# Added rows kept in PSUM for the product with att, two shorter last batches, and one block as the last group of nodes

## The chip, the cores and the metric

The kernel runs on one core of a Trainium2 chip, in one launch. A core has TensorE (PE, with its weight loads shown apart as PEld), VectorE (DVE), ScalarE (ACT), GpSimd (POOL) and SyncE (SP), each with a queue of its own that it works through in order, and 16 DMA engines. The metric is the device time of an execution in microseconds; three runs are shown before, and one further execution was profiled.

## The reference

Two layers of message passing over a graph of 6250 nodes and 206250 edges sorted by destination (100000 edges, their reverses and a loop at each node), with a layer norm after each. The change lies in the first layer, GATv2 attention with 8 heads of 16 features:

```python
def gatv2(x, edge_index, edge_attr, W_l, b_l, W_r, b_r, W_e, att, b_att):
    src, dst = (edge_index[0], edge_index[1])
    xl = (x @ W_l + b_l).reshape(-1, H, O)
    xr = (x @ W_r + b_r).reshape(-1, H, O)
    ee = (edge_attr @ W_e).reshape(-1, H, O)
    m = jax.nn.leaky_relu(xl[src] + xr[dst] + ee, NEG_SLOPE)
    logits = jnp.einsum('eho,ho->eh', m, att)
    lmax = jax.ops.segment_max(logits, dst, num_segments=N)
    exl = jnp.exp(logits - lmax[dst])
    denom = jax.ops.segment_sum(exl, dst, num_segments=N)
    alpha = exl / (denom[dst] + 1e-16)
    msg = xl[src] * alpha[:, :, None]
    out = jax.ops.segment_sum(msg, dst, num_segments=N)
    return out.reshape(-1, H * O) + b_att
...
h = layer_norm(x + attn_out, g1, be1)
ffn = jax.nn.gelu(h @ W1 + b1, approximate=False) @ W2 + b2
return layer_norm(h + ffn, g2, be2)
```

The second layer gathers node features for each edge, multiplies them with filters made from edge attributes by a small network, and sums them by destination.

## The kernel before

**Tiling.** Edges are cut into 269 units of 768 (`TU` = 6 tiles of 128). For each unit, `load` (L394) has POOL gather six tiles of the source rows `xl` from the table `fXL` by indirect DMA (`gather`, L364), and SP load the edge attributes `ea`, the places `lb` and three rows `xr`. `xl` has 19 buffers. A head's 16 features stand beside a 17th column (`OW` = 17): the table's linear part, 0.2 of the sum over the features times att, so that leaky_relu's product with att is max(z, 0) times 0.8 att, summed over the features, plus that column.

**One unit's logits.** `terms(u, half)` (L413) lets PE add the edge term, the destination term and, for half 0 alone, the gathered rows (a product with the identity, L423) in a PSUM tile `z` of one half, three tiles. The pool `zp` has three such buffers (L387). Half 0 ends with an ACT copy of the linear column from `z` to `pr` (L426). `parts(u)` (L430) is DVE's: for half 0 the product max(z, 0) times `attb` from `z` to `pr` (L439); for half 1 first the sum of `z` and the gathered rows, written to `pr` (L436), then the product from `pr` to `pr` (L439). `logits` (L441) sums over the 17 columns.

**Batches.** Maxima by destination need scans along the edges, done for a batch of units at once with (unit, head) as partitions. Batches are of 3, 4 and 6 units and then of 8 (`HEAD`, `U`, `fast_plan` L57); each has an `end`, the step of its last unit's logits. `rows` transposes the logits (step end + 1), `peaks` scans (end + 2), `shifts` and `weights` make the exponentials (end + 3), and from step end + 4 on (end + 3 for the last batch) each of its units is given a step by the table `when` (L560): `messages` multiplies the rows by them on DVE, `sums` (one step later) sums them by destination on PE and has ACT copy the result to `sb` (L542, L543), `sum_up` and `collect` (two and three steps later) add it to `acc`. In the last 28 steps a step may take two units.

**Order.** The whole is under a manual schedule: each engine runs its instructions in the order in which the loop (L580 to L611) calls the functions. In step k that is: load(k + 2); terms(k + 1, 0); sum_up; terms(k + 1, 1); shifts and weights, or peaks, where due; sums; parts(k); places(k + 2), DVE's one-hot of the destinations; logits(k); collect; the one-hot and messages of the units of this step; rows where due; and a piece of the node work.

**Nodes.** When all edges into a group of node blocks (128 nodes each) are collected, `nodes` (L635) normalises them, runs the feed-forward network and three layer norms, and writes the second layer's table `fFEAT`. There are 25 groups for 49 blocks: one of one block, then 24 of two (`cuts`, L62). A group is a generator of 19 pieces; `Queue.step` (L93) advances the groups at work by one piece each, at most two groups (two lanes), the second counted from the first that hasn't ended. It is called once a step, twice from step 273 on; `rest` runs what is left after the last step. The second layer (`convolution`, L746) begins with a memset of its accumulator on POOL, in the place of `acc`, and with gathers from `fFEAT`.

Of the kernel before, what the change touches and what calls it, by code (L numbers as in the profile page):

```python
# [11 lines left out]
AF = mybir.ActivationFunctionType  # L12
OP = mybir.AluOpType
# [19 lines left out]
U = 8  # L33
# [4 lines left out]
H = 8  # L38
O = D // H
OW = O + 1  # L40
ZW = H * OW
G = 2
SPREAD = 6
HEAD = (3, 4)
RAW = 4
ENDING = 28
EB = 8
# [2 lines left out]
def fast_sizes(n_nodes, n_edges):  # L50
    nt = -(-n_edges // P)
    nu = -(-nt // TU)
    up = -(-nu // P) * P
    return nu, up, -(-(n_nodes + 1) // P) * P


def fast_plan(n, e):  # L57


    nu, _, np_ = fast_sizes(n, e)  # L60
    nb = np_ // P
    cuts = [0, *range(nb % G or G, nb + 1, G)]  # L62
    groups = [(b, c - b) for b, c in zip(cuts, cuts[1:])]
    done, need = [], [0] * nu
    for b, g in groups:
        q = min((b + g) * P / n, 1.0)
        u = min(nu - 1, int((q * e + SPREAD * math.sqrt(e * q * (1 - q))) / UE + 0.5))
        done.append(u)
        if u + 1 < nu:
            need[u + 1] = max(need[u + 1], (b + g) * P)  # L70
    head = HEAD if nu > sum(HEAD) else ()
    left = nu - sum(head)
    rest = (left % U,) if left % U else ()
    batches, u, end = [], 0, -2
    for m in head + rest + (U,) * (left // U):
        u += m
        end = max(u - 1, end + 2)
        batches.append((u - m, m, end))
    return groups, done, need, batches
# [28 lines left out]
class Fast:  # L108
# [88 lines left out]
    def tables(self, acc, xlp):  # L197
# [28 lines left out]
        with tc.tile_pool(name="tb1", bufs=1) as t1, tc.tile_pool(name="tb2", bufs=2) as t2, \  # L226
                tc.tile_pool(name="tbp", bufs=4, space=PSUM) as tp, \
                tc.tile_pool(name="trp", bufs=2, space=PSUM) as rp:
            xgs = []
            for u in range(min(RAW, NU)):  # L230
                xg = t1.tile([P, TU, D], F32, name="xg", bufs=RAW)
                for t in range(TU):
# [145 lines left out]
    def attention(self, acc, xlp, xls):  # L378
# [3 lines left out]
        tc, nc, a, NU = self.tc, self.nc, self.a, self.NU  # L382
        with ExitStack() as st:
# [7 lines left out]
            ohs, eas, zs, prs, lgs, ms, sbs, nds = {}, {}, {}, {}, {}, {}, {}, {}  # L391
            ws = {"last": (H, last)}

            def load(u):  # L394
                if u >= RAW:
                    xls[u] = xlp.tile([P, TU, ZW], F32, name="xl")
# [16 lines left out]
            def terms(u, half):  # L413
                ea, _, xr = eas[u]
                xl, oht = xls[u], ohs[u]
                z = zs[u, half] = zp.tile([P, 3 * ZW], F32, name="z")
                for lhs, rhs in ((ea, self.w3[:, 2]), (oht, xr)):
                    for t in range(3):
                        e = slice((3 * half + t) * P, (3 * half + t + 1) * P)
                        nc.tensor.matmul(z[:, t * ZW:(t + 1) * ZW], lhs[:, e], rhs,  # L420
                                         start=(t == 0 and lhs is ea), stop=(half == 1 and t == 2 and lhs is oht))
                if half == 0:
                    nc.tensor.matmul(z, self.ident, xl[:, :3, :].rearrange("p t f -> p (t f)"),  # L423
                                     start=False, stop=True)
                    prs[u] = wk.tile([P, TU * H, OW], F32, name="pr")
                    nc.scalar.activation(prs[u][:, :3 * H, O], z.rearrange("p (h o) -> p h o", o=OW)[:, :, O], AF.Copy)  # L426
                else:
                    del eas[u], ohs[u]

            def parts(u):  # L430

                for k in range(2):
                    z = zs.pop((u, k)).rearrange("p (h o) -> p h o", o=OW)
                    p = prs[u][:, 3 * H * k:3 * H * (k + 1)]
                    if k:
                        nc.vector.tensor_add(p.rearrange("p h o -> p (h o)"), z.rearrange("p h o -> p (h o)"),  # L436
                                             xls[u][:, 3:, :].rearrange("p t f -> p (t f)"))
                        z = p
                    nc.vector.scalar_tensor_tensor(p[:, :, :O], z[:, :, :O], 0.0, self.attb, op0=OP.max, op1=OP.mult)  # L439

            def logits(u):  # L441
                b, i = of[u]
# [46 lines left out]
            def shifts(b):  # L489

                R, hb, pk, cr = ws[b]
                gd = b1.tile([R8, UE], F32, name="gd")
                for s in (slice(0, UE // 2), slice(UE // 2, UE)):
                    nc.vector.scalar_tensor_tensor(gd[:R, s], hb[:R, s], cr[:R], pk[:R, s], op0=OP.add, op1=OP.max)
                sc = b2.tile([R8, 1], F32, name="sc")
                nc.vector.tensor_scalar(sc[:R], cr[:R], gd[:R, 0:1], 0.0, op0=OP.subtract, op1=OP.min)
                nc.scalar.activation(sc[:R], sc[:R], AF.Exp)
                sd = b2.tile([R8, U], F32, name="sd")
                nc.scalar.activation(sd[:R], self.bmask[:R], AF.Copy, scale=sc[:R])
                ws[b] = R, gd, sd  # L500

            def weights(b):
                R, gd, sd = ws[b]
                lg = lgs.pop(b)
                ex_ps = mp.tile([P, TU, R], F32, name="m")
                nc.tensor.matmul(ex_ps, self.ident, lg[:, :, :R], start=True, stop=False)
                for t in range(TU):
                    nc.tensor.matmul(ex_ps[:, t, :], gd[:R, t * P:(t + 1) * P], self.negi[:R, :R],
                                     start=False, stop=(t == TU - 1))
                ex = b2.tile([P, TU, R8], F32, name="ex")  # L510
                nc.scalar.activation(ex[:, :, :R], ex_ps, AF.Exp)  # L511
                for i in range(R // H):
                    xv = xls[self.batches[b][0] + i].rearrange("p t (h o) -> p t h o", o=OW)
                    nc.scalar.activation(xv[:, :, :, O], ex_ps[:, :, i * H:(i + 1) * H], AF.Exp)
                s_ps = mp.tile([P, U], F32, name="m")
                nc.tensor.matmul(s_ps, self.e128[:R], sd[:R], start=True, stop=True)
                s = b2.tile([P, U], F32, name="s", bufs=3)
                nc.scalar.activation(s, s_ps, AF.Copy)  # L518
                ws[b] = ex, s
# [37 lines left out]
                nc.vector.scalar_tensor_tensor(v, v, ws[b][1][:, i:i + 1], nds.pop(u), op0=OP.mult, op1=OP.add)  # L557


            when, ready, k = {}, 0, 0  # L560
            for u in range(NU):
                end = self.batches[of[u][0]][2]
                k = max(k, end + (4 if end < NU - 1 else 3))
                busy = {k - 2, k - 3} & {b[2] for b in self.batches}
                if len(when.get(k, ())) == (2 if k >= NU or k > NU - ENDING and not busy else 1):
                    k += 1
                when.setdefault(k, []).append(u)

            AHEAD = 2
            ends = {end: b for b, (_, _, end) in enumerate(self.batches)}  # L570
            for u in range(min(AHEAD, NU)):
                load(u)
                places(u)
            for half in range(2):
                terms(0, half)
            for k in range(max(when) + 4):
                now, sums_of, ups_of, got = (when.get(k - i, []) for i in range(4))
                if k + AHEAD < NU:
                    load(k + AHEAD)
                if k == 2:  # L580
                    nodes = Queue(self.nodes(st, acc), self.done, 2)
                if k + 1 < NU:
                    terms(k + 1, 0)
                if ups_of:
                    sum_up(ups_of)
                if k + 1 < NU:
                    terms(k + 1, 1)
                if k - 3 in ends:
                    shifts(ends[k - 3])
                    weights(ends[k - 3])  # L590
                if k - 2 in ends:
                    peaks(ends[k - 2])
                for u in sums_of:
                    sums(u)
                if k < NU:
                    parts(k)
                cs = [nc.vector.value_load(self.r0[0:1, u:u + 1], min_val=0, max_val=self.n) for u in got]
                if k + AHEAD < NU:
                    places(k + AHEAD)
                if k < NU:  # L600
                    logits(k)
                for u, c in zip(got, cs):
                    collect(u, c)
                for u in now:
                    ohs[u] = self.one_hot(wk, u)
                    messages(u)
                if k - 1 in ends:
                    rows(ends[k - 1])
                for _ in range(1 + (k > NU + 3) if k > 1 else 0):
                    nodes.step(max(got, default=-1))  # L610
            nodes.rest()  # L611
# [1024 lines left out]
```

## Time and profile before

| | us |
|---|---|
| runs | 4414.8, 4415.79, 4425.34 (median 4415.79) |
| the profiled execution | 4420.11, its span 4418.2 |
| first logits, last logits (L445) | 125.6, 2247.8 |
| gathers of the first layer | 45.3 to 2241.4 |
| first gather of the second layer | 2329.8 |

| engine | busy us over the span | share |
|---|---|---|
| PE | 3545.6 | 80% |
| DVE | 2581.9 | 58% |
| ACT | 963.3 | 22% |
| POOL | 3333.3 | 75% |

Times are counted from the start of the span. A row of the timeline has the start, the duration, engine, line, operation, what is written from what, a count, and in brackets the idle time of the engine before it with what ended it. A row of a group has the count, the busy time and the mean of one in ns, and the idle time before with its releasers. A row of waits has the total, the number and the longest. The chain of work that ended last is put down to POOL for 31%, to DMA and to PE for 20% each and to DVE for 11% of the span. Mean granted clock of TensorE: 0.829 of full speed.

### The profile page before, as it was taken

The page shows a single profiled execution, that of the slowest core. Times are in us where ns is not written, and L with a number is a line of the kernel's source. Part 1 is how long each engine was busy: PE and PEld are TensorE (multiplying, and loading weights), DVE is VectorE, ACT ScalarE, POOL GpSimd, SP SyncE. Part 2 cuts the span into 40 slices and gives each one's busy share as a digit, 9 for nine tenths or more (in the row PEclk, how much of TensorE's full clock was granted, in tenths as well). Part 3 has the DMA queues.
Part 4 walks back from the last instruction along what each step waited for, and adds up shares of the span by engine and source line. Part 5 has one row for each costly group of instructions (what it writes and reads, how often), then busy time and mean ns, then how long its engine had stood idle before and what let it go on. Part 6 is the DMA issues. An engine that isn't in the chain of part 4 may idle for free.

```text
span 4418.2 us, 67000 instructions
## 1 busy us (share of the span) xinstructions
PE 3545.6 (80%) x21381; PEld 2843.6 (64%) x21381; DVE 2581.9 (58%) x6023; ACT 963.3 (22%) x2528; POOL 3333.3 (75%) x3236
## 2 busy tenths in 40 slices
PE   7787777777677777777768888888888888888887
PEld 5665566566566656555646776677676767766776
DVE  5786676666676666666754444444444444444444
ACT  3122222222222222222242111111111211111111
POOL 6777777777777777777746777777777777777776
PEclk7787777888877787778778889888888888898987
DMA  7654444444444444444512222222222222222222
GB/s 206 176 153 120 130 129 124 128 131 127 127 128 126 129 130 127 126 123 132 134 42 64 60 60 57 60 61 59 61 59 61 61 59 57 59 61 61 60 60 49
DMA packets 290617, 428.21 MB, mean 97 GB/s; under 512 B 122701, under 2 KB 199455, under 8 KB 290255
## 3 DMA queue, kind: packets, MB, share of 16 engines
q0 software_dynamic: 103296, 218.27, 20.3%
q1 hardware_dynamic: 183258, 197.74, 14.9%
q10 hardware_dynamic: 3700, 7.82, 0.5%
q8 instruction: 173, 2.83, 0.3%
q14 instruction: 190, 1.55, 0.1%
HBM read 403.55 MB, written 19.96 MB: 96 GB/s over the span
## 4 chain that ended last, share of the span: by engine, by line
POOL 31%; DMA 20%; PE 20%; issue 15%; DVE 11%; ACT 1%; DVEq 1%; ACTq 0%; SPq 0%; POOLq 0%
POOL f L366 21%; DMA xl<-fXL,fsrc 10%; POOL xl L366 9%; DMA f<-fFEAT,fsrc 8%; PE z L420 6%; PE z L423 3%; DVE f L833 2%; PE m L538 2%; PE y L852 2%; PE m L551 1%; DVE f L829 1%; DVE pr L439 1%; DVE os L825 1%; PE y L850 1%; DVE xl L528 1%
## 5 line engine op out<-in xcount | busy, mean ns | idle before, releaser
L366 POOL DMA_INDIRECT xl<-fXL,fsrc x1590 | 1711.8, 1077 | 487.3 <-issue 401.9
L366 POOL DMA_INDIRECT f<-fFEAT,fsrc x1614 | 1577.2, 977 | 506.5 <-issue 443.7
L852 PE MATMUL y<-os,f 128*128 128x96 f32 x3228 | 774.8, 325 | 10.2
L850 PEld LDWEIGHTS y<-os,f 128*128 128x128 f32 x3228 | 551.3, 208 | 353.2 <-DVE f L833 301.5
L829 DVE TENSOR_TENSOR f<-w,f 128x256 f32<-128x256 f32 x405 | 171.6, 424 | 982.0 <-DMA f<-fFEAT,fsrc 973.2
L850 PE MATMUL y<-os,f 128*128 128x32 f32 x3228 | 583.5, 264 | 198.1 <-DVE f L833 197.7
L420 PE MATMUL z<-fw,ea 128*128 128x136 f32 x3228 | 622.6, 340 | 64.9 <-DVE pr L439 55.7
L803 ACT ACTIVATE h<-h_ps 128x384 f32<-128x384 f32 x540 | 265.2, 491 | 1647.1 <-PE h_ps L802 1647.0
L423 PE MATMUL z<-xl,fcst 128*128 128x408 f32 x538 | 317.0, 678 | 364.0 <-DMA xl<-fXL,fsrc 363.7
L420 PEld LDWEIGHTS z<-fw,ea 128*128 128x128 f32 x3228 | 535.1, 237 | 114.1 <-DVE pr L439 56.3
L852 PEld LDWEIGHTS y<-os,f 128*128 128x128 f32 x3228 | 538.5, 209 | 31.5 <-DVE f L833 30.6
L809 PE MATMUL w<-wq,h 128*128 128x256 f32 x1620 | 498.3, 437 | 0.0
L833 DVE TENSOR_TENSOR f<-w,f 128x384 f32<-128x384 f32 (+1 forms) x810 | 408.7, 546 | 0.0
L423 PEld LDWEIGHTS z<-xl,fcst 128*128 128x128 f32 x538 | 99.6, 231 | 390.2 <-issue 316.3
L809 PEld LDWEIGHTS w<-wq,h 128*128 128x128 f32 x1620 | 317.0, 217 | 30.8
L825 DVE TENSOR_TENSOR os<-oh,e 128x512 f32<-128x512 f32 x405 | 280.2, 692 | 64.6 <-PE y L852 26.7
L538 PE MATMUL m<-xl,oh 128*32 128x136 f32 x3228 | 226.9, 349 | 72.4 <-ACT s L518 55.3
L436 DVE TENSOR_TENSOR pr<-z,xl 128x408 f32<-128x408 f32 x269 | 154.7, 575 | 209.9 <-DMA xl<-fXL,fsrc 117.7
L528 DVE TENSOR_TENSOR xl<-xl,ex 128x384 f32<-128x384 f32 x538 | 273.6, 548 | 4.0 <-ACT ex L511 4.0
L551 PEld LDWEIGHTS m<-fcst,sb 128*128 128x128 f32 x1076 | 204.1, 240 | 109.5 <-issue 104.7
L445 DVE TENSOR_REDUCE lg<-pr 128x48 f32<-128x816 f32 x269 | 266.5, 991 | 1.8 <-DVE pr L439 1.8
L802 PE MATMUL h_ps<-h,m 128*128 128x384 f32 x540 | 263.0, 622 | 0.0
(145 smaller groups left out, 4152.8 us busy)
## 6 DMA issues: line engine op xcount, KB each, us to landing
ea<-fast_eat_dram SPq DMA_DIRECT2D x269, 384.0 KB
lb<-fLB SPq DMA_DIRECT2D x269, 144.0 KB
f<-fFEAT,fsrc POOLq DMA_INDIRECT x1614
xl<-fXL,fsrc POOLq DMA_INDIRECT x1590
xr<-fXR SPq DMA_DIRECT2D x807, 8.5 KB
e<-fast_e8t_dram SPq DMA_DIRECT2D x16, 384.0 KB
fXR<-pt SPq DMA_DIRECT2D x16, 306.0 KB
fXL<-tb SPq DMA_DIRECT2D x16, 204.0 KB
```

The source lines that it names most:

```text
L366: self.nc.gpsimd.indirect_dma_start(out=to, out_offset=None, in_=table, in_offset=bass.IndirectOffsetOnAxis(ap=self.src[:, g:g + 1], axis=0))
L420: nc.tensor.matmul(z[:, t * ZW:(t + 1) * ZW], lhs[:, e], rhs, start=(t == 0 and lhs is ea), stop=(half == 1 and t == 2 and lhs is oht))
L423: nc.tensor.matmul(z, self.ident, xl[:, :3, :].rearrange("p t f -> p (t f)"), start=False, stop=True)
L445: nc.vector.tensor_reduce(lgs[b][:, :, i * H:(i + 1) * H], prs.pop(u).rearrange("p (t h) o -> p t h o", h=H), axis=mybir.AxisListType.X, o ...
L528: nc.vector.tensor_mul(v, v, ws[b][0][:, t:t + 3, i * H:(i + 1) * H, None].to_broadcast([P, 3, H, O]))
L538: nc.tensor.matmul(ag[q * W:(q + 1) * W], oh[:, t, :], xl[:, t, :], start=(t < 4), stop=(t + 4 >= TU))
L803: nc.scalar.activation(h[:, s], ps, AF.Gelu_apprx_tanh, scale=sc)
L809: nc.tensor.matmul(w[:, 2 * t:2 * t + 2, :], hs[p][:, e:e + P], wq, start=True, stop=True)
L825: nc.vector.tensor_mul(os[:, own], oh.rearrange("p t u w -> p (t u) w")[:, own, None, :].to_broadcast([P, n, 4, W]), e4s[p][:, at, :, None ...
L833: nc.vector.tensor_mul(vy[:, :, j, 32:].rearrange("p t (c x) -> p t c x", c=3), w[:, :, None, 64 + j * 32:96 + j * 32].to_broadcast([P, n, ...
L850: nc.tensor.matmul(ys[p][:, i, 0], vy[:, e, 0], os[:, e, 3], start=(c == t == i == 0), stop=False)
L852: nc.tensor.matmul(ys[p][:, i, 1:], vy[:, e, 1], os[:, e, :3], start=False, stop=last)
```

## The change

In `parts`, DVE adds the gathered rows of half 1 to `z` in PSUM and writes the sum back there. The linear column of half 1 is then copied by ACT from `z`, as that of half 0 was (`linear`, now called for both halves), and both products read `z`. The last two batches are of 5 and 3 units (`TAIL`), so that 36 take the place of 35; the last one's `rows`, `peaks` and `weights` come a step earlier, counted from its end, than those of the others, and the table `when` is made accordingly. The last group of nodes has one block, the 24 before it two.

```diff
+TAIL = (5, 3)
...
-    cuts = [0, *range(nb % G or G, nb + 1, G)]
+    cuts = [0, *range((nb - 1) % G or G, nb, G), nb]
...
-    head = HEAD if nu > sum(HEAD) else ()
-    left = nu - sum(head)
+    head, tail = (HEAD, TAIL) if nu > sum(HEAD + TAIL) else ((), ())
+    left = nu - sum(head + tail)
     rest = (left % U,) if left % U else ()
     batches, u, end = [], 0, -2
-    for m in head + rest + (U,) * (left // U):
+    for m in head + rest + (U,) * (left // U) + tail:
...
-                    nc.scalar.activation(prs[u][:, :3 * H, O], z.rearrange("p (h o) -> p h o", o=OW)[:, :, O], AF.Copy)
+                    linear(u, 0)
...
+            def linear(u, k):
+
+                z = zs[u, k].rearrange("p (h o) -> p h o", o=OW)
+                nc.scalar.activation(prs[u][:, 3 * H * k:3 * H * (k + 1), O], z[:, :, O], AF.Copy)
+
             def parts(u):
 
+                z = zs[u, 1]
+                nc.vector.tensor_add(z, z, xls[u][:, 3:, :].rearrange("p t f -> p (t f)"))
+                linear(u, 1)
                 for k in range(2):
                     z = zs.pop((u, k)).rearrange("p (h o) -> p h o", o=OW)
-                    p = prs[u][:, 3 * H * k:3 * H * (k + 1)]
-                    if k:
-                        nc.vector.tensor_add(p.rearrange("p h o -> p (h o)"), z.rearrange("p h o -> p (h o)"),
-                                             xls[u][:, 3:, :].rearrange("p t f -> p (t f)"))
-                        z = p
-                    nc.vector.scalar_tensor_tensor(p[:, :, :O], z[:, :, :O], 0.0, self.attb, op0=OP.max, op1=OP.mult)
+                    nc.vector.scalar_tensor_tensor(prs[u][:, 3 * H * k:3 * H * (k + 1), :O], z[:, :, :O], 0.0,
+                                                   self.attb, op0=OP.max, op1=OP.mult)
...
-            when, ready, k = {}, 0, 0
+            when, k = {}, 0
+            due = {end + (end < NU - 1): b for b, (_, _, end) in enumerate(self.batches)}
             for u in range(NU):
                 end = self.batches[of[u][0]][2]
-                k = max(k, end + (4 if end < NU - 1 else 3))
-                busy = {k - 2, k - 3} & {b[2] for b in self.batches}
+                k = max(k, end + (4 if end < NU - 1 else 2))
+                busy = {k - 1, k - 2} & set(due)
...
-                if k - 3 in ends:
-                    shifts(ends[k - 3])
-                    weights(ends[k - 3])
-                if k - 2 in ends:
-                    peaks(ends[k - 2])
+                if k - 2 in due:
+                    shifts(due[k - 2])
+                    weights(due[k - 2])
+                if k - 1 in due:
+                    peaks(due[k - 1])
...
-                if k - 1 in ends:
-                    rows(ends[k - 1])
+                if k in due:
+                    rows(due[k])
```

More of the change, by code (lines that the diff above doesn't have):

```diff
@@ L569, in attention @@
             AHEAD = 2
-            ends = {end: b for b, (_, _, end) in enumerate(self.batches)}
             for u in range(min(AHEAD, NU)):
```

## The prediction

> **What bounds the kernel now.** I read the page's busy table first, then the groups of the first layer, then who waits for whom on DVE and PE between 300 and 2240 us, and last the order of time there and at the end of the layer. In the table by stretches the columns are the window, its length, then PE, PEld, DVE, ACT and POOL busy.
>
> ```profile
> 300.00:2240.00 1940.00, 1456.54 (x10074) 1157.57 (x10075) 1325.32 (x2990) 494.30 (x1577) 1510.24 (x1411) 0.80 0.47 127
> L366 POOL DMA_INDIRECT xl<-fXL,fsrc x1411 | 1511.6, 1071 | 430.1 <-issue 351.1 <-PE z L420 17.7 <-DMA xl<-fXL,fsrc 8.8
> PE z L423 <- DMA xl<-fXL,fsrc: 363.7, 154, 6.4
> PE z L420 <- DVE pr L439: 37.0, 25, 2.6
> DVE pr L439 <- ACT pr L426: 108.3, 82, 4.1
> ```
>
> POOL has 1411 gathers in 1940 us and never idles longer than its fixed 0.30 us between two: 1071 + 304 ns each, six to a unit, 8.25 us per unit. PE and DVE wait for what the gathers land (PE 363.7 us). So gathers set the pace, and the 235 steps (1411 / 6) cost DVE only 1325.32 / 235 = 5.64 us each. The fourth line says that the terms of unit k+1's second half wait for unit k's first product: `zp` has three buffers. The fifth says that a product of DVE waits for the ACT copy of the linear column of the same half, although the two write different columns; over the stage the shortest gap from the end of that copy to the product is 0.03 us.
>
> The order of one step, from the timeline:
>
> ```profile
> 1210.36 0.21 ACT L426 ACTIVATE pr<-z 128x24 f32<-128x24 f32 x1 [0.45 <-PE z L423]
> ...
> 1212.10 0.52 DVE L439 SCALAR_TENSOR_TENSOR pr<-z,fattb 128x384 f32<-128x384 f32 x1
> ...
> 1212.55 0.56 DVE L436 TENSOR_TENSOR pr<-z,xl 128x408 f32<-128x408 f32 x1
> ...
> 1212.68 1.20 PE L420 MATMUL z<-fw,ea 128*128 128x136 f32 x6 [2.05 <-DVE pr L439]
> 1213.15 0.56 DVE L439 SCALAR_TENSOR_TENSOR pr<-pr,fattb 128x384 f32<-128x384 f32 x1
> ...
> 1214.98 1.12 PE L538 MATMUL m<-xl,oh 128*32 128x136 f32 x12 [0.25 <-ACT cr L485]
> ...
> 1216.21 0.28 ACT L542 ACTIVATE sb<-m 128x128 f32<-128x128 f32 x1 [1.28 <-PE m L538]
> ```
>
> The second product (1213.15) follows the add at once, long before PE's sums of the step (1214.98) and ACT's `sb` copies (1216.21). Nothing on ACT holds DVE there.
>
> **The change, part by part.**
>
> *1. The add stays in PSUM.* Add, product, product replace product, add, product. The second product reads `z` instead of `pr`: by its sister's row 546 for 562 ns, -0.02 us. An add that writes PSUM is in no row. Its ends are the product from `z` over 384 columns (0.55) and the reduce over 816 (0.99); I take its own row with the other destination, 0.58, nearest in shape. The ends are worth -0.03 and +0.41 us a step.
>
> *2. A second copy of the linear column, on ACT: 0.21 us (row L426).* As busy time it is nothing, ACT being busy 494 of 1940 us. But its place decides. `linear(u, 1)` is called in `parts(k)`, after `sums` of the same step, and ACT runs in program order: it stands behind the two `sb` copies, these wait for PE's sums, these stand behind `terms(k+1, 1)`, and those wait for the first product of step k. The second product, behind the copy as L439 is behind L426 today, cannot start until all of it is through. On DVE everything else of the step is queued behind that product: the one-hot of unit k+2, logits, collect, one-hot, messages, the nodes' pieces, and the next add and first product, which release PE again. A ring closes in each step, and DVE idles in it between its two products for:
> - first product to PE 0.06 (1212.62 to 1212.68)
> - second half's terms 549.9 / 471 + 188.5 / 471 = 1.57 (groups L420 of 2826 and 1413, six and three a half)
> - sums 202.2 / 238 = 0.85 (group L538, 2856 = 238 x 12)
> - PE to ACT 0.11 (1216.10 to 1216.21), `sb` pair 0.44 (1216.21 to 1216.65; L543's row is 1216.38, 0.27), copy 0.21, ACT to DVE 0.03
>
> That is 3.27, less about 0.1 where PE's groups overlap: 3.2 us. A step with `weights` adds its PE and ACT work to the ring, from the groups of that window: 31.1 / 29 + 50.6 / 29 (L506, L508) + 0.48 + 1.70 + 0.17 (L511, eight of L514, L518) - 0.85 for the sums that run beside = 4.3 us, over 8 units 0.54. A step with `peaks` adds 0.84 (1214.14 to 1214.98), 0.10 a unit. One unit then takes 5.64 + 3.2 + 0.54 + 0.10 = **9.48 us, more than the gathers' 8.25**. The bound changes: POOL fills the four `xl` buffers that it has to spare (19 against 15 live) and then waits.
>
> The cover today is also worth something at the start: logits of unit 0 are at 125.6 us and those of unit 268 at 2247.8, 7.89 us a unit, because the first thirty steps run faster than the gathers on loads made ahead. That is lost too. New: 269 x 9.48 = 2550, less 22 for the seven steps among the first thirteen that have no sums (3.2 each) and 18 for 23 early steps without node work (206 us of DVE node groups / 269 = 0.77 each): 2510. Last logits at 2636 instead of 2248: **+388 us**.
>
> [...]
>
> *3. What POOL gains.* Counted over the timeline, 151 of the 1411 gathers begin while a second product runs, and together last 21.6 us more than at the median of 944 ns; beside the first product, which reads PSUM, the excess is nil. With POOL no longer the bound, this is worth nothing; if it stays the bound, -22 us. [...]
>
> *4. Batches of 5 and 3.* One batch more before the last logits: 4.0 of scans (L471 to L477), 1.2 of `shifts`, 4.3 + 0.8 in the ring, +10. After them, today:
>
> ```profile
> 2251.16 0.60 PE L462 MATMUL m<-fcst,lg 128*64 128x128 f32 x4
> ...
> 2263.65 1.03 DVE L528 TENSOR_TENSOR xl<-xl,ex 128x384 f32<-128x384 f32 x2 [4.05 <-ACT ex L511]
> ...
> 2293.68 21.23 POOL L761 MEMSET acc<- 128x6304 f32 x4 [52.26 <-PE n L676]
> 2329.81 0.95 POOL L366 DMA_INDIRECT f<-fFEAT,fsrc  x1 [14.90 <-DMA fBASE<-h]
> ```
>
> 12.5 us (2251.16 to 2263.65) pass with one batch alone; now messages of the five lie beside it, though its scans and weights still take about 9 in the same queues, and two steps fall away, one with work of its own: -5. From the last collect (ends 2292.1) to the second layer's first gather 37.7 us pass, through the last group's chain.
>
> *5. Last group one block.* The chain's PE, DVE and ACT pieces halve in width: two L702 of 2.08, L710 3.57, L733 2.07, three L632 of 0.88, statistics and adds: about -9.5. But the node queue has two lanes. By the new due units group 22 starts at step 267 and has 12 of its 19 pieces behind it when the steps end; group 24 may not start until it is through, seven rounds later. Sixteen rounds now take 31 us (2293.6 to 2324.6), so +13.6. Together +4. The memset (21.2 us) stays covered: it starts with the last group's first matmuls, and 22 us of chain and 5 of landing follow.
>
> **Sum:** 388 + 10 - 5 + 4 = +397 us; I take +390, since waits now in DVE's busy stretches may fall into the idle ones. The profiled execution has 4420.11 us (span 4418.2 and 1.9 around it), 4.3 above the median of the three runs, 4415.79: 4810 by the profile, **4805 by the median**.
>
> **Rivals.**
> *The ring stays open, or fits* (chance 0.12). If the product doesn't wait for the copy, or the ring is shorter than 8.25 us, gathers stay the bound: 4416 - 22 - 5 + 4 + 5 (the added batch, half hidden) = 4398, faster. It decides where a unit takes under 8.25, 1.2 less than my sum. For it: the idle time of DVE today, 2.6 us a step, is nearly the ring's 3.2. Against: the 108.3 us row, and in-order ACT.
> *A ring at full clock* (0.10). PE's granted clock is 0.80 in the stage. In the fast stretches the second half's terms take 1.12 (1230.51 to 1231.63) and sums 0.66: idle 2.5, weights 0.51, 8.73 a unit, 4620. For it: PE will be less busy. Against: stretches with less PE work had no higher clock (0.66 from 2240 to 2330).
> *Only the tail counts* (0.03): the two layers as before, tail -1 to +8: 4416 to 4424.
> *A dear PSUM add* (0.05): +0.41 a step, 4915. Half clock throughout would be 10.4 a unit and 5050.
>
> **How the numbers follow.** My forecast has 0.70, 4660 to 4910. The range takes in the full-clock rival and the dear add: 4600 to 4930, about 0.83. This kernel can be told from no change at some 0.3%, 13 us. Faster 0.10, same 0.04 (the last two near-unchanged cases and the unlucky edge of the first), slower 0.86.
>
> **What would show it.** Right: the copy twice as often (538); the second product waiting for ACT some 3 us per step; PE's 363.7 us of waits for gathers nearly gone; POOL idle beyond 0.30 us, released by PE's sums; POOL's share in the first layer down from 78% to about 68%; last group's first matmuls some rounds after the last collect. Wrong: POOL still without a wait, a unit in 8.25 us or less, or a second product that starts right behind the first.

## The result, and the profile after

| | before | after |
|---|---|---|
| median of four runs, us | 4417.93 (4414.80 to 4425.34) | 4888.34 (4874.83 to 4906.12) |
| ratio | 1 | 1.1064 (95%: 1.1021 to 1.1108) |
| span of the profiled execution, us | 4418.2 | 4895.2 |
| first logits, last logits, us | 125.6, 2247.8 | 116.2, 2723.8 |
| one unit, from the logits of unit 60 to those of unit 240, us | 8.28 | 9.98 |
| last logits to the second layer's first gather, us | 82.0 | 91.7 |
| from there to the end, us | 2088.4 | 2079.7 |

The change costs 470 us. Between the two profiles the span grows by 477.0: the stretch from the first to the last logits by 2607.6 - 2122.2 = 485.4, the piece after it by 9.7, while the time before the first logits and the second layer take 9.5 and 8.7 less. The last two are not the change's: a second pair of executions on another chip (the last experiment) has 115.0 before and 117.2 after for the first, 2082.1 and 2080.5 for the second. So the loss lies in the first layer's steps.

The table by stretches of the kernel after, with the columns as in the prediction:

```profile
300.00:2600.00 2300.00, 1618.43 (x9926) 1252.87 (x9924) 1303.47 (x2950) 521.41 (x1780) 1496.74 (x1392) 0.71 0.39 107
```

At 9.98 us a unit, 2300 us are 230.4 steps. POOL is busy 65% of them (78% before), DVE 1303.47 / 230.4 = 5.66 us a step, as before (5.64). PE's granted clock is 0.71, where it was 0.80. The groups of the same stretch, kernel after:

```profile
L367 POOL DMA_INDIRECT xl<-fXL,fsrc x1392 | 1496.7, 1075 | 806.0 <-ACT pr L434 399.4 <-issue 329.6 <-ACT sb L548 12.4
L421 PE MATMUL z<-fw,ea 128*128 128x136 f32 x2796 | 609.3, 371 | 509.9 <-DVE pr L443 500.2 <-issue 9.4
L443 DVE SCALAR_TENSOR_TENSOR pr<-z,fattb 128x384 f32<-128x384 f32 x466 | 256.3, 551 | 945.1 <-ACT pr L434 942.7 <-issue 2.4
L543 PE MATMUL m<-xl,oh 128*32 128x136 f32 x2784 | 210.6, 366 | 16.9 <-ACT s L523 7.2 <-ACT cr L490 6.9 <-ACT sb L548 2.9
L421 PE MATMUL z<-xr,oht 96*128 96x136 bf16 x1398 | 205.5, 269 | 0.0
L439 DVE TENSOR_TENSOR z<-z,xl 128x408 f32<-128x408 f32 x232 | 134.3, 579 | 0.8 <-PE z L424 0.4
L434 ACT ACTIVATE pr<-z 128x24 f32<-128x24 f32 x466 | 98.8, 212 | 418.1 <-PE z L424 345.7 <-DVE h L719 21.3 <-DVE xl L533 12.6
```

The gathers last as long as before (1075 ns for 1071), but POOL now idles 806 us beside them. The add that writes PSUM takes 579 ns; the one that wrote SBUF took 576. Waits of the same stretch, kernel after (total, number, longest):

```profile
DVE pr L443 <- ACT pr L434: 942.7, 229, 11.4
ACT sb L547 <- PE m L543: 668.1, 229, 8.0
PE z L421 <- DVE pr L443: 500.2, 330, 7.8
POOL xl L367 <- ACT pr L434: 399.4, 115, 16.3
```

Read from the top: once a step (229 of 230) DVE waits with a product for ACT's copy of the linear column; ACT waits with its `sb` copies for PE's sums; PE waits with the terms for a product of DVE. That is a closed ring. PE's wait for gathered rows, 363.7 us before, no longer appears. POOL waits for the ring; by the profile its long waits end with ACT's column copy. One turn of it in the timeline of the kernel after:

```profile
1224.86 0.54 DVE L443 SCALAR_TENSOR_TENSOR pr<-z,fattb 128x384 f32<-128x384 f32 x1
1225.45 1.73 PE L421 MATMUL z<-fw,ea 128*128 128x136 f32 x6 [3.67 <-DVE pr L443]
1226.97 0.55 PE L421 MATMUL z<-xr,oht 96*128 96x136 bf16 x3
...
1228.29 1.12 PE L543 MATMUL m<-xl,oh 128*32 128x136 f32 x12 [0.25 <-ACT cr L490]
...
1229.46 0.28 ACT L547 ACTIVATE sb<-m 128x128 f32<-128x128 f32 x1 [1.22 <-PE m L543]
1229.63 0.27 ACT L548 ACTIVATE sb<-m 128x128 f32<-128x128 f32 x1
1229.79 0.22 ACT L434 ACTIVATE pr<-z 128x24 f32<-128x24 f32 x1
1230.04 0.56 DVE L443 SCALAR_TENSOR_TENSOR pr<-z,fattb 128x384 f32<-128x384 f32 x1 [4.64 <-ACT pr L434]
```

The first product ends at 1225.40, PE starts the next unit's second half 0.05 us later, then come two small products of a step with `peaks`, the sums, the two `sb` copies, the column copy, and 0.03 us after it the second product. Three engines take turns, and DVE stands still for 4.64 us.

The end of the layer, kernel after:

```profile
2768.10 0.60 DVE L562 SCALAR_TENSOR_TENSOR acc<-acc,s,m 128x64 f32 x2 [1.31 <-issue]
...
2785.09 0.39 PE L680 MATMUL n<-fcst,acc 128*128 128x8 f32 x2 [0.93 <-DVE h L742]
2785.75 21.23 POOL L766 MEMSET acc<- 128x6304 f32 x4 [137.89 <-PE n L681]
2815.50 0.95 POOL L367 DMA_INDIRECT f<-fFEAT,fsrc  x1 [8.52 <-issue]
```

Everything is collected at 2768.70; the last group's first products start only 16.4 us later, released by a node instruction of another group (L742). Before, the memset that follows these products started 1.6 us after the last collect (2292.1 to 2293.7).

### The profile page after: what moved, and what is told of

Its sections match the earlier page's. It is cut to its first block, busy times and chain, and to the rows that moved or that the text cites. A ratio compares the mean times of both kernels' runs of the same rounds, so it can differ in the third digit from the quotient of the medians.

```text
span 4895.2 us, 67029 instructions
## 1 busy us (share of the span) xinstructions
PE 3763.0 (77%) x21407; PEld 2978.3 (61%) x21407; DVE 2578.7 (53%) x6030; ACT 1004.2 (21%) x2805; POOL 3323.3 (68%) x3236
## 4 chain that ended last, share of the span: by engine, by line
POOL 19%; issue 8%; DVE 8%; DMA 8%; PE 7%; ACT 1%; DVEq 1%; POOLq 0%; ACTq 0%
POOL f L367 19%; DMA f<-fFEAT,fsrc 8%; DVE f L838 2%; PE y L857 1%; PE z L421 1%; DVE f L834 1%; DVE os L830 1%; PE m L543 1%; PE y L855 1%; DVE xl L533 1%; PE ps L916 1%; DVE pr L443 1%; DVE lg L450 1%; PE w L814 1%; PE h_ps L807 0%
## 5 line engine op out<-in xcount | busy, mean ns | idle before, releaser
L367 POOL DMA_INDIRECT xl<-fXL,fsrc x1590 | 1705.6, 1073 | 899.2 <-ACT pr L434 421.8
L421 PE MATMUL z<-fw,ea 128*128 128x136 f32 x3228 | 700.7, 370 | 602.6 <-DVE pr L443 567.5
L421 PEld LDWEIGHTS z<-fw,ea 128*128 128x128 f32 x3228 | 587.4, 258 | 711.0 <-DVE pr L443 611.4
L443 DVE SCALAR_TENSOR_TENSOR pr<-z,fattb 128x384 f32<-128x384 f32 x538 | 295.8, 550 | 1072.0 <-ACT pr L434 1069.5
L424 PE MATMUL z<-xl,fcst 128*128 128x408 f32 x538 | 340.9, 726 | 0.0
L807 PE MATMUL h_ps<-h,m 128*128 128x384 f32 x540 | 280.4, 658 | 0.0
L533 DVE TENSOR_TENSOR xl<-xl,ex 128x384 f32<-128x384 f32 x538 | 273.0, 546 | 0.0
L543 PE MATMUL m<-xl,oh 128*32 128x136 f32 x3228 | 245.3, 369 | 22.9 <-ACT s L523 8.4
L421 PE MATMUL z<-xr,oht 96*128 96x136 bf16 x1614 | 236.6, 268 | 1.5 <-DVE pr L443 1.2
```

The source lines that it names most:

```text
L367: self.nc.gpsimd.indirect_dma_start(out=to, out_offset=None, in_=table, in_offset=bass.IndirectOffsetOnAxis(ap=self.src[:, g:g + 1], axis=0))
L443: nc.vector.scalar_tensor_tensor(prs[u][:, 3 * H * k:3 * H * (k + 1), :O], z[:, :, :O], 0.0, self.attb, op0=OP.max, op1=OP.mult)
L533: nc.vector.tensor_mul(v, v, ws[b][0][:, t:t + 3, i * H:(i + 1) * H, None].to_broadcast([P, 3, H, O]))
L543: nc.tensor.matmul(ag[q * W:(q + 1) * W], oh[:, t, :], xl[:, t, :], start=(t < 4), stop=(t + 4 >= TU))
```

## The experiments

One caution first. The first four runs, the next four and the two after them were made on three other chips, on which the kernel before itself took 5399, 5352 and 5404 us (19, 35 and 17 runs). There a unit takes 9.4 to 9.7 us even where no ring closes (9.66 with `copy_first`). Ratios below are always to the kernel before on the same chip, and are the estimates on record with their 95% intervals, which are not exactly the quotients of the two medians (5699.24 / 5398.93 is 1.056, the estimate 1.0597). The times in us that the first expectations name were meant for a kernel before of 4418 us; on these chips only ratios and waits can be set against them. What is different on these chips is taken up at `loose_ring`.

**The products alone (psum_alone) and the plan alone (plan_alone).** The first is the change's hunks in `terms` and `parts`, the second all the others.

```diff
+                z = zs[u, 1]
+                nc.vector.tensor_add(z, z, xls[u][:, 3:, :].rearrange("p t f -> p (t f)"))
+                linear(u, 1)
```

```diff
+TAIL = (5, 3)
...
+    cuts = [0, *range((nb - 1) % G or G, nb, G), nb]
...
+            due = {end + (end < NU - 1): b for b, (_, _, end) in enumerate(self.batches)}
```

> The kernel before with the edit of parts alone: add into PSUM, ACT copy of half 1's column, both products from z; batches and groups as before. Ring theory (the second product waits for a copy that stands on ACT behind the sb copies of the step): nearly the whole loss stays, 4860 to 4890 us, DVE idle before the product from z by some 4 us per step, released by ACT. Plan theory (the batches of 5 and 3 and the last group cost the time): 4410 to 4425.

> The kernel before with the batches of 5 and 3, the earlier last batch and the last group of one block, and parts as before. Ring theory: the first layer keeps the pace of the gathers (8.25 us a unit) and only the end changes, -5 to +15 us, 4413 to 4433. Plan theory: 4850 to 4890.

The products alone: 5699.24 us for 5398.93, ratio 1.0597 (1.0548 to 1.0647), 10.78 us a unit. The plan alone: 5406.46, ratio 1.0032 (1.0004 to 1.0061). The loss is the products'. It is smaller than expected: 300 us here, where nearly all of 470 had been expected, since a unit takes longer here without the ring, too. Groups and waits between 600 and 2600 us, products alone:

```profile
L438 DVE TENSOR_TENSOR z<-z,xl 128x408 f32<-128x408 f32 x185 | 107.1, 579 | 0.7 <-PE z L423 0.3
```

```profile
DVE pr L442 <- ACT pr L433: 811.8, 154, 11.4
```

2000 us are 185.5 steps: 811.8 / 185.5 = 4.4 us a step of DVE waiting for ACT, in the same place, and again a PSUM add of 579 ns.

**The same with the copy at another place in ACT's queue (copy_first).** The add and the copy are called at the head of the step, so that the copy stands on ACT ahead of the `sb` copies.

```diff
-            def parts(u):
+            def added(u):
                 z = zs[u, 1]
                 nc.vector.tensor_add(z, z, xls[u][:, 3:, :].rearrange("p t f -> p (t f)"))
                 linear(u, 1)
+
+            def parts(u):
...
+                if k < NU:
+                    added(k)
```

> As psum_alone, but the add and the copy of half 1's column are called first in the step, ahead of the next unit's terms, so that on ACT the copy stands ahead of everything of its step; the operations and their number are the same. Ring theory: the ring is open, gathers set the pace again, less what POOL gains where the second product no longer reads two operands from SBUF (21.6 us by my count): 4385 to 4420. PSUM theory (an add that writes PSUM, or two products that read it beside PE, are themselves dear): stays at 4800 or more.

5384.10 us, ratio 0.9972 (0.9939 to 1.0005), 9.66 us a unit: the loss is gone on this chip, with the same instructions and the same PSUM add. The add has moved to the head of the step together with the copy; in `column_by_dve`, below, it stays where it was. Waits between 600 and 2600 us:

```profile
DVE pr L445 <- ACT pr L433: 316.6, 85, 13.0
```

DVE's wait for ACT falls from 4.4 to 316.6 / 207 = 1.5 us a step. A repetition on a third chip gave 0.9981 (0.9956 to 1.0005), 5392.60 for 5404.35:

> The earlier run of this kernel (the added rows stay in PSUM, and the column copy goes to ACT ahead of its copies of the sums; old plan of batches and groups) was on a chip where the kernel before took 5399 us, and its ratio was 0.9972. This run asks whether that holds where the gathers bound the first layer, as in the profile of before (8.28 us a unit, POOL 76%). Ring theory (the copy's place in ACT's queue closes the ring, nothing else in the product edit costs): the loss of 390 us is gone; at a kernel before of 4418 us this one takes 4390 to 4425 (ratio 0.994 to 1.002), a gain at most the 22 us that the gathers lose beside the old second product. PSUM theory (a slower add or product in PSUM): DVE's step stays longer by 0.1 to 0.3 us, the ratio is 1.00 to 1.02 with DVE's wait for ACT gone. Capacity theory (the copy on ACT is late whatever its place): ratio above 1.05.

It was meant to show whether the 22 us that gathers lose beside the old second product come back. It cannot: this chip, too, was one where the gathers don't bound the layer. Both intervals hold 1, so no version measured here is faster than the kernel before, and what `copy_first` does at 4418 us, whether it gains or even gets back all of the 470 us, was not measured.

**The ring without PSUM (ring_in_sbuf).** The add goes to `pr` in SBUF, as before, but ACT copies two columns of it onto themselves (258 ns for the 212 of the one column) ahead of the second product, at the place where the change has its copy; the product must wait for ACT with no write to PSUM by DVE.

```diff
+                p = prs[u][:, 3 * H:]
+                z = zs[u, 1].rearrange("p (h o) -> p h o", o=OW)
+                nc.vector.tensor_add(p.rearrange("p h o -> p (h o)"), z.rearrange("p h o -> p (h o)"),
+                                     xls[u][:, 3:, :].rearrange("p t f -> p (t f)"))
+                nc.scalar.activation(p[:, :, O - 1:], p[:, :, O - 1:], AF.Copy)
```

> The add goes to pr in SBUF as before and the second product reads pr as before, but the add stands ahead of both products and ACT copies two columns of pr in place (features 15 and the linear one) between add and second product, at the place that the new column copy has. Nothing writes PSUM but PE. Ring theory: the ring closes the same, 4830 to 4910, pace 9.6 to 10 us a unit. PSUM theory: as before, 4410 to 4430.

5678.95 us, ratio 1.0542 (1.0481 to 1.0602), 10.72 us a unit, on the same chip as the products alone (10.78). Waits between 600 and 2600 us:

```profile
DVE pr L440 <- ACT pr L436: 822.4, 155, 11.0
POOL xl L366 <- ACT pr L436: 468.4, 144, 11.1
```

Nearly all of the loss is there without the PSUM add. The theory that PSUM accesses are dear falls; a wait at this place is enough.

**The whole change with the copy first (change_copy_first), and the column copied by DVE (column_by_dve).** The first adds the diff of `copy_first` to the change. The second has the products of the change with DVE in ACT's place, so that no copy of the second half crosses engines:

```diff
-                linear(u, 1)
+                zv = z.rearrange("p (h o) -> p h o", o=OW)
+                nc.vector.tensor_copy(prs[u][:, 3 * H:, O], zv[:, :, O])
```

> The changed kernel whole, but with the add and the copy of half 1's column called first in the step, as in copy_first. Ring theory: the loss is gone; what is left is the plan's part (0 to +0.4%, the last group waits for a lane) less POOL's gain (0 to -0.5%): ratio 0.995 to 1.004. If the plan and the PSUM edit only cost together: 1.05 or more.

> As psum_alone (batches and groups as before), but DVE itself copies half 1's linear column from z, between add and products, some 0.1 to 0.3 us a unit; ACT has no second copy. Ring theory: no engine but DVE stands between add and second product, the ring is open, ratio 0.993 to 1.003. PSUM theory: as psum_alone, 1.05 or more.

5355.64 for 5351.61, ratio 1.0009 (0.9984 to 1.0034), and 5358.08, ratio 1.0012 (0.9976 to 1.0048). On this chip, either way of taking the copy out from behind the sums removes the whole loss. One more DVE instruction a step (199 ns in its group) costs nothing that can be told here.

**The two halves of the plan (groups_alone, batches_alone).** First the one block as the last group, with the old batches; then the batches of 5 and 3 with their due steps, with the old groups.

```diff
+    cuts = [0, *range((nb - 1) % G or G, nb, G), nb]
```

```diff
+TAIL = (5, 3)
...
+            due = {end + (end < NU - 1): b for b, (_, _, end) in enumerate(self.batches)}
```

> The kernel before with only the cuts changed (last group of nodes one block). Lane theory (a group may start only when the group before the last has ended): the last group starts 3 rounds of the rest after the last collect, some 6 us late, and is some 9 us shorter: -6 to +3 us at the end, ratio 0.998 to 1.001; its first matmuls (L676) come 4 to 8 us after the last collect. Without a lane effect they come at once, as in the kernel before, and the end is 9 us shorter.

> The kernel before with only the batches of 5 and 3 and the earlier last batch; cuts as before. From last logits to last collect 4 to 10 us less than before (44.2 us), last group's first matmuls at most 3 us after the last collect; against it one more batch before the last logits (0 to +10). Ratio 0.998 to 1.002.

Groups: 5357.18, ratio 1.0018 (0.9996 to 1.0041); batches: 5368.20, ratio 1.0027 (1.0006 to 1.0048). The end of the layer with the groups alone:

```profile
2774.36 0.60 DVE L557 SCALAR_TENSOR_TENSOR acc<-acc,s,m 128x64 f32 x2 [1.30 <-issue]
...
2785.79 0.29 PE L675 MATMUL n<-fcst,acc 128*128 128x8 f32 x2
2785.94 0.31 PE L676 MATMUL n<-fcst,acc 128*128 128x128 f32 x1
2786.36 21.23 POOL L761 MEMSET acc<- 128x6304 f32 x4 [111.05 <-PE n L676]
```

From the end of the last collect to the memset pass 11.4 us with the groups alone, 8.5 with the batches alone, 17.0 with both (the plan alone), and 1.0 with neither (`copy_first`). I had expected the last group's first products 4 to 8 us after the collect with the groups alone (2785.79 - 2774.96 = 10.8) and the start within 3 us with the batches alone. The batches alone were also expected to bring the last collect 4 to 10 us nearer to the last logits than the 44.2 us of the kernel before; it is 45.5. Each half of the plan alone delays the last group; neither gains anything.

**The copy where only the reduce waits for it (loose_ring).** The kernel before, with a copy of the same column after the second half's add, in place. Both products go ahead; the sum over the columns has to wait for ACT.

```diff
                         z = p
+                        nc.scalar.activation(p[:, :, O], p[:, :, O], AF.Copy)
                     nc.vector.scalar_tensor_tensor(p[:, :, :O], z[:, :, :O], 0.0, self.attb, op0=OP.max, op1=OP.mult)
```

> The kernel before, with one more ACT copy of the second half's column (in place, after the second product, of what the sum over the columns reads): only the reduce at the end of the products waits for it, not the second product. Ring theory: a copy of the same size, late in the same queue of ACT, costs little where the second product doesn't wait for it, since the ring then spans the reduce and its followers alone: 8.3 to 8.9 us a unit where the kernel before has 8.28, ratio 1.00 to 1.03. Rival (any more work of ACT between the two products costs the same, as ACT's queue itself is the bound): ratio 1.05 to 1.10, as with the product edit alone (1.06).

5592.31 for 5404.35, ratio 1.0371 (1.0319 to 1.0423), 10.39 us a unit: between the two bands, so both expectations miss. The timeline:

```profile
1239.71 0.57 DVE L436 TENSOR_TENSOR pr<-z,xl 128x408 f32<-128x408 f32 x1
...
1240.31 0.56 DVE L440 SCALAR_TENSOR_TENSOR pr<-pr,fattb 128x384 f32<-128x384 f32 x1
...
1242.59 0.66 PE L539 MATMUL m<-xl,oh 128*32 128x136 f32 x12
...
1245.89 0.28 ACT L543 ACTIVATE sb<-m 128x128 f32<-128x128 f32 x1 [4.30 <-PE z L420]
1246.07 0.27 ACT L544 ACTIVATE sb<-m 128x128 f32<-128x128 f32 x1
1246.22 0.24 ACT L439 ACTIVATE pr<-pr 128x24 f32<-128x24 f32 x1
...
1246.50 1.00 DVE L446 TENSOR_REDUCE lg<-pr 128x48 f32<-128x816 f32 x1 [5.07 <-ACT pr L439]
```

The second product follows the add at once (1240.28 to 1240.31), though ACT's copy into another column of the same `pr` is still to come: writing `pr` together makes no wait. In the change, the product and the copy also share `z`, and there the product waits (942.7 us in 229 waits). By elimination, that leaves the shared PSUM tile as the reason; why sharing it puts the two in order was not shown.

The ring is not open, though. The reduce waits, and with it all that stands behind it in DVE's queue, the next first product among it, which releases PE:

```profile
DVE lg L446 <- ACT pr L439: 858.3, 190, 9.8
```

Between 600 and 2600 us these are 192.5 steps, so DVE waits 858.3 / 192.5 = 4.5 us a step, as long as with the products alone. What is gained is the second product, which now goes ahead of the wait. A unit takes 10.39 us where it takes 9.68 with the copy first on the same chip (`copy_first_again`), 0.71 more; the products alone cost 10.78 - 9.66 = 1.12.

The rest of the turn shows what is different on these chips. PE's last recorded matmul of the sums ends at 1243.25, and ACT starts the `sb` copy only at 1245.89, 2.64 us later. Counted between 300 and 2200 us, the pair starts more than 1 us after both the sums and ACT's previous instruction in 116 of 182 steps of this run, 316.8 us in all or 1.74 a step. The seven other runs on these chips, in which no ring closes, have it as well: 50 to 59% of the steps and 2.2 to 2.7 us a step (493.4 us over 196 steps in `copy_first`). With the second product in the ring it is less, 62.5 us over 175 steps with the products alone and 98.5 over 176 with the ring in SBUF. In the kernel before and the kernel after, on the chips where the former takes 4418 or 4409 us, it never happens. In the waits of `copy_first` between 600 and 2600 us it stands as one that the profile can put down to nothing ("remote"):

```profile
ACT sb L549 <- remote: 392.3, 48, 20.0
```

In one such stretch PE has no record from 748.3 to 761.8 us, while POOL's gathers go on, most of them 1.25 us apart. These late starts can't be subtracted from a unit: `copy_first` would be left with 9.66 - 2.52 = 7.1 us, less than its six gathers take, 6 x (1.07 + 0.30) = 8.2. So these chips tell which place of the copy closes a ring, but not what a ring costs where the gathers are the bound. Whether the sums end later there than the records say, or their signal arrives later, isn't settled.

**Both kernels once more (change_again, before_again).**

> The whole change, unaltered, on a chip where the kernel before takes about 5400 us, beside which the parts were run. If the parts add (product edit alone 1.0597, plan alone 1.0032): ratio 1.063 (1.055 to 1.071), and 10.7 to 10.9 us a unit in the first layer, since the ring is the same and only the floor under it is higher here. Rival: the parts strengthen one another (the ring met by last batches of other sizes), as the first measurement's 1.106 would have it if it held on every chip: ratio 1.09 to 1.11.

> The kernel before, unaltered, for its trace on such a chip. If the floor is higher here because every step of the first layer loses time to waits that the ring does not cause, the unit is 9.5 to 9.8 us (as with the copy placed first, 9.66) instead of 8.28, the gathers' mean stays at 1.06 to 1.09 us, POOL is idle between gathers for over 900 us instead of 484, and second-layer time is 2500 us instead of 2088. Rival: the gathers themselves are slower here: their mean is 1.25 us or more and POOL is as full as before (over 75%).

Neither expectation could be tested, since this chip ran the kernel before in 4408.98 us (7 runs). It gave a second measurement of the result instead: 4881.41 us (4 runs), ratio 1.1054 (1.1014 to 1.1094); a unit 9.93 for 8.25. Waits between 600 and 2600 us, kernel after on this chip:

```profile
DVE pr L443 <- ACT pr L434: 812.2, 199, 11.1
PE z L421 <- DVE pr L443: 439.0, 285, 7.8
```

The first execution has 821.4 and 437.8 us there. Whether the parts add up to the whole cannot be checked on one chip from these runs: the parts were measured where a unit costs 9.66 us without the ring, the whole where it costs 8.28.

## Why the prediction was right, and where its sizes were off

**What bounds the kernel, and the ring.** Right. The forecast was that the column copy, in order behind the sums, closes a ring through DVE, PE and ACT and takes the bound from the gathers. The profile has its waits, and the copy's place in ACT's queue decides: 1.0597 behind the sums, 0.9972 ahead of them, the same instructions on the same chip. One sign came otherwise: POOL's waits were to be ended by PE's sums, and the profile puts them down to ACT's column copy (399.4 us).

**The length of a unit** is the term that was mis-sized: 9.48 us forecast, 9.98 measured. The parts, with the 230.4 steps of the stretch:

| us a step | forecast | measured |
|---|---|---|
| DVE's own work | 5.64 | 1303.47 / 230.4 = 5.66 |
| DVE's wait for ACT at the second product | 3.2 + 0.54 + 0.10 = 3.84 | 942.7 / 230.4 = 4.09 |
| DVE's other idle time | 0 | (2300 - 1303.47 - 942.7) / 230.4 = 0.23 |

Of the 0.25 us in the wait, PE explains most: by the groups above the terms of one half now take (609.3 + 205.5) / 466 = 1.75 us instead of 1.57, and the sums of a unit 210.6 / 232 = 0.91 instead of 0.85. I had priced PE's part at the clock of before (0.80), and the new schedule was granted 0.71. The 0.23 us, 54 in the stretch, are for the most part (43 us) gaps of under 0.15 us between DVE's instructions, which a sum of busy times leaves out.

**The early steps.** 40 us were taken off for steps without sums or node work; 268 x 9.98 - 2607.6 = 67 us is what the unit's steady pace overstates. So the last logits come 476 us later than before, not 388.

**The PSUM add** was put at the duration of the SBUF add, 0.58 us a step, between -0.03 and +0.41 of cost. It takes 0.579, and the ring without it costs nearly the same (1.0542 for 1.0597, with overlapping intervals): the value taken was right and the rival of a dear add falls.

**Full clock** was given a tenth, because PE would be less busy. The opposite came: 0.71. The reason given against it, that less PE work had not meant a higher clock before (0.66 from 2240 to 2330 us), was the right one to weigh more.

**An open ring** falls with the same lines. **Only the tail counts** falls with the 470 us.

**POOL's gain** of 21.6 us, called worth nothing if POOL is no longer the bound, went to nothing in another way, too: the gathers' mean is 1073 ns over the layer for 1077 before. Beside the products, which now read PSUM, the 264 gathers that begin there last 946 ns, but 212 begin beside the messages (L533, two inputs from SBUF) and last 1571 ns.

**The plan** was put at +10 - 5 + 4 = +9 us. The added batch (+10) ahead of the last logits can't be told from the ring. The piece behind them is 9.7 us longer (9.2 in the second pair of profiles), where -1 had been forecast:

| us | before | after | change, forecast | change, measured |
|---|---|---|---|---|
| last logits to last collect | 44.2 | 44.9 | -5 | +0.7 |
| last collect to memset (wait for a lane) | 1.6 | 17.0 | +13.6 | +15.4 |
| memset to first gather (the last group's chain) | 36.1 | 29.8 | -9.5 | -6.4 |

That the last group would wait for a lane was right, and nearly its size. The 5 us that the shorter last batches were to save never came, and the narrower chain saved two thirds of what was forecast. The plan alone costs 0.32% (0.04 to 0.61%) on its chip. What was not seen is that the batches alone make the last group wait as well.

**The sum.** Between the profiles it is 477 us for 397 forecast. The stretch of the logits is 97 us longer than forecast and the end 11; the added batch's 10 don't show, and the start and the second layer took 18 us less, which is luck, since it isn't the change's.

## What to carry to other kernels

A small instruction is not priced by its duration but by what stands ahead of it in its engine's queue: a 0.21 us copy behind two copies that wait for PE cost 9.98 - 8.28 = 1.7 us a step. Issued ahead of them it cost nothing that could be measured, on chips where a step takes 9.66 us anyway. Where an engine is 25% busy and "free", ask what the last instruction ahead of the new one waits for, and whether that comes back to the consumer of the new one; if it does, add up the whole turn and compare it with the pace of today's bound. A plan that gives the last stage less work gains only if the stage can also start: look for the lane, not only for the length of the work.

## What the runs showed of the hardware

The granted clock fell from 0.80 to 0.71 when PE's busy share fell from 75% to 70%, though PE's idle stretches over 3 us became fewer, from 25 to 17 in 1000 us (23 to 20 in the second pair of executions). That speaks against the full-clock rival, which had less PE work lift the clock. What sets the clock was not shown.

The same kernel before took 4418 and 4409 us on two chips and 5352 to 5404 on three others, with a second layer of 2082 to 2088 us on the former and 2505 to 2517 us (both `copy_first` runs) on two of the latter. The first logits come at 232 to 236 us there instead of 115 to 126. Single instructions of DVE and ACT last as long (the product from `z` 548 ns in `copy_first` and 546 in the kernel before, ACT's `h<-h_ps` 491 in both); the time lies between them, among other places between PE's sums and ACT's copy (493.4 / 196 = 2.52 us a step in `copy_first`). Its cause is open.
